# Layer 1 of a two-layer cross-attention kernel: two pairs of subtiles at a time, three of the seven half products split once more, softmax by head on ACT, in a fixed order

## The chip, the cores and the metric

The kernel runs on one core of a Trainium2 chip. A core has a matrix engine (TensorE, PE in the profile, with PEld for its weight loads), a vector engine (VectorE, DVE), a scalar engine (ScalarE, ACT), a general engine (GpSimd, POOL) and SyncE (SP), which here only issues transfers. Each engine runs its own instructions in order and waits on semaphores for the others. Operands lie in SBUF, matmul results in PSUM (eight banks of 512 float32 columns for 128 partitions). The metric is device time in microseconds, the median of several executions. One execution was also taken with the hardware profiler.

## The reference

Four batches of 1024 tokens of width 1024 go through two cross-attentions with 64 keys each. Cut to what matters:

```python
# layer 0: 32 query heads, 8 key heads of 32
out = softmax(q k^T / sqrt(32) + mask0) v          # 64 keys
x = layernorm((out @ Wo + bo) + x) * gamma0 + beta0
# layer 1: 16 heads of 64
a = layernorm(ctx) * gamma1 + beta1
scores = (x @ Wq.T) (a @ Wk.T)^T / 8               # 64 keys for each head, masked
out = softmax(scores) (a @ Wv.T) @ Wo.T
y = x + tanh(gate) * out
```

All of it is float32. As there are 16 heads of 64 keys, the scores of a token are again 1024 numbers. For each batch b the kernel folds Wq with the keys into one matrix ad[b] (1024 x 1024) and the values with Wo and the gate into bd[b] (1024 x 1024). Layer 1 is then, for 128 tokens at a time: s = x ad[b] + key_bias, a softmax over each of the 16 groups of 64 columns, and y = x + p bd[b].

## The kernel before

The 4096 tokens are 32 subtiles of 128, taken as 16 pairs. After layer 0's attention (to 681.5 us) comes layer 0's output projection, one pair after the other ("the wo stage", 681.5 to 1126.3 us), and then layer 1 (1126.3 to 1905.4 us): for each pair a score project with ad and an output project with bd.

A project multiplies 256 tokens x 1024 by 1024 x 1024 with the Strassen-Winograd scheme: the left side is four blocks of 128 tokens x 512, the right side four of 512 x 512, and seven block products take the place of eight. The left sums S1 to S4 are made by `left_out` (L429 to L432, four DVE additions of 128 x 512), the right sums T1, T2, T3, N4 by `right_sums` (L183 to L186, DVE, 128 x 2048) once for each batch. `products` (L446 the matmuls) makes each product as four K-steps of 128 x 128 x 512; the trace shows two PE records for each K-step, so 8 records a product and 56 a project. DVE takes each product from PSUM into the rows r or s (L455; L459 where the key bias is added). Products that share a bank go on adding to it after DVE has taken what it held: order X1, X6, V7, X5, X3, V4, W2, with four banks "wx" (128 x 512) and two double banks "big".

`project` puts a list of other steps ("fill") between the seven products: softmax steps, turns of the next rows, right sums. A scheduler then orders each engine's instructions, and can move PE's matmuls past one another.

The softmax of a subtile is `softmax_front` (L493 row maximum by head, L498 its floor, L501 subtraction, all on DVE, and L502 one exponential of 128 x 1024 on ACT) and `softmax_back` (L511 sum and L512 reciprocal by head, L516 division, on DVE). The rows are stored to p1 in DRAM on ACT's queue and come back as pq in a layout of quarters (`load_quarters`, ACT's queue), which DVE turns in 32 x 32 blocks (`turn_quarters`, L419). The rows x of layer 1, written to x1 in DRAM by `close_rows` of the wo stage (layer normalisation L292 to L309), come back on SP's queue as xq and are turned likewise. Pairs 0 and 15 of p are turned at once by PE transposes instead (L407) with ACT copies (L414). y is stored on SP's queue.

In the wo stage, POOL adds bo to the residual rows of each pair (L962), except for the first ones, which DVE does (L1099); bo is loaded in `other_work`, during layer 0's attention.

Of the kernel before, what the change touches and what calls it, by code (L numbers as in the profile page):

```python
# [14 lines left out]
P = 128  # L15
# [56 lines left out]
def tile_two_cross_attentions(  # L72
# [35 lines left out]
    ps_wx = ctx.enter_context(tc.tile_pool(name="ps_wx", bufs=4, space=bass.MemoryType.PSUM))  # L108
    ps_big = ctx.enter_context(tc.tile_pool(name="ps_big", bufs=2, space=bass.MemoryType.PSUM))
# [133 lines left out]
    mask1_sb = constant(mask1.partition_broadcast(P), [P, B, S], "mask1", U8)  # L243
# [401 lines left out]
    def load_queries(t):  # L645
        q = qpool.tile([P, KC, P], F32, tag="q", name=f"q0_{t}")
        nc.sync.dma_start(out=q, in_=qTd[t // SUB][:, :, sub_ap(t % SUB)])

        m = small.tile([P, 2, S], F32, tag="m0", name=f"m0_{t}", bufs=2)
        for e in range(2):  # L650
            nc.sync.dma_start(out=m[:, e], in_=mask0[sub_ap(t), :])
        queries[t] = q, m
# [313 lines left out]
    def other_work(rows):  # L966

        nonlocal fold, early, bo_sb, w_o, first, first_rows, second
# [20 lines left out]
        bo_sb = constant(bo0.partition_broadcast(P), [P, H], "bo", F32, fold)  # L989
# [50 lines left out]
    def open_stage():  # L1040
        nonlocal lpool, o2pool, rpool, gamma0_sb, beta0_sb
# [5 lines left out]
        gamma0_sb, beta0_sb = (  # L1047
            constant(ap.partition_broadcast(P), [P, H], n, F32, c2)
            for ap, n in ((gamma0, "gamma0"), (beta0, "beta0"))
# [16 lines left out]
    lefts = {}  # L1066

    def load_x1(pair):
        xq = xqpool.tile([P, 2 * NQ, QW], F32, tag="xq", name=f"xq1_{pair}")
        load_quarters(xq, x1[pair])  # L1070
        return xq

    def turn_x1(pair, xq, pool=None, tag="xT"):

        xT = (pool or xTpool).tile([P, KC, 2 * P], F32, tag=tag, name=f"xT_{pair}")

        def half(h):
            turn_quarters(xq, xT[:, h * HK : (h + 1) * HK, :], (h * HK, (h + 1) * HK))

        def blocks():  # L1080
            lefts[pair] = left_out(xT, lpool if pool else lxpool, f"x_{pair}")

        return [lambda: half(0), lambda: half(1), blocks]
# [18 lines left out]
    for pair in range(1, NPAIR):  # L1102
# [7 lines left out]
        if pair == KC + 2:  # L1110
            w_a, w_a_sums = right_weight(ad[0], "wb", "a0", True)
        if pair in (NPAIR - 3, NPAIR - 2):
            fill += w_a_sums[0:2] if pair == NPAIR - 3 else w_a_sums[2:4]
        if pair == 3:
            early_cm.close()
            xTpool = open_pool(last_cm, "x1T", 1)
            lxpool = open_pool(last_cm, "leftx", 1)
            xqpool = open_pool(last_cm, "x1q", 1)
        if pair == NPAIR - 4:
            xq = load_x1(1)  # L1120
        if pair == NPAIR - 3:
            fill += turn_x1(1, xq)

        def tail():
# [3 lines left out]
            else:  # L1128
                turned[2]()
# [3 lines left out]
        if pair == NPAIR - 2:  # L1133
            xq = load_x1(0)
            turned = turn_x1(0, xq, o2pool, "o2")
            fill = turned[:2] + fill
    w_b, w_b_sums = right_weight(bd[0], "wa", "b0", True)
    xq = load_x1(2)
    run(fill)
    stage.close()  # L1140


    spool = open_pool(last_cm, "scores1", 4)
    pqpool = open_pool(last_cm, "p1q", 1)
    scores = {}

    def score(pair, fill):
        if pair:
            s = [spool.tile([P, H], F32, tag="s", name=f"s1_{pair}_{u}") for u in range(2)]
        else:  # L1150
            both = o2pool.tile([P, 2, H], F32, tag="o2", name="s1_0")
            s = [both[:, u] for u in range(2)]
        project(lefts.pop(pair), w_a, s, fill, key_bias[:, pair // PPB, :])
        scores[pair] = [su.rearrange("p (h s) -> p h s", s=S) for su in s]

    def softmax1(pair):

        s = scores[pair]
        steps = []
        if pair in (0, NPAIR - 1):  # L1160
            at_once[pair] = pqpool.tile([P, 2, H], F32, tag="pq", name=f"pn_{pair}")
        for u in range(2):
            steps += softmax_front(s[u], True, f"1_{pair}_{u}", pair == 0)
        for u in range(2):
            total, divide = softmax_back(
                s[u], f"1_{pair}_{u}", at_once[pair][:, u] if pair in at_once else None
            )

            def end(u=u, total=total, divide=divide):
                total()  # L1170
                divide()
                if pair not in at_once:
                    nc.scalar.dma_start(
                        out=p1[pair][sub_ap(u), :], in_=s[u].rearrange("p h s -> p (h s)")
                    )

            steps.append(end)
        return steps

    def new_pT(pair):  # L1180
        return ppool.tile([P, KC, 2 * P], F32, tag="pT", name=f"pT1_{pair}")

    def turn_at_once(pair):
        pT = new_pT(pair)
        del scores[pair]
        for u in range(2):
            turn(at_once[pair][:, u], pT[:, :, sub_ap(u)])
        return left_out(pT, lppool, f"p_{pair}")

    probs1 = {}  # L1190
    at_once = {}

    def turn_p(pair):

        scores.pop(pair)
        pq = pqpool.tile([P, 2 * NQ, QW], F32, tag="pq", name=f"pq_{pair}")
        load_quarters(pq, p1[pair], nc.scalar)
        pT = new_pT(pair)

        def half(h):  # L1200
# [100 lines left out]
```

## Time and profile before

Runs: 1908.11, 1907.85 and 1911.4 us, median 1908.11. The profiled execution is one further execution; its span from first to last instruction is 1909.7 us, 1.6 us (0.1%) over that median, so its own time is taken as the span.

| stretch | us | PE busy | DVE busy | ACT busy | POOL busy | granted PE clock |
|---|---|---|---|---|---|---|
| whole span of the profiled execution | 1909.7 | 1865.5 | 1290.2 | 427.4 | 178.5 | 0.994 |
| wo stage, 681.5 to 1126.3 | 444.8 | 436.9 | 289.9 | 56.9 | 78.4 | 1.00 |
| layer 1, 1126.3 to 1905.4 | 779.1 | 777.6 | 508.1 | 39.3 | 0.0 | 1.00 |
| middle of layer 1, 1200 to 1600 | 400.0 | 400.0 | 263.4 | 16.9 | 0.0 | 1.00 |

How to read the lines below: the page's first part has each engine's busy time, its share of the span and its instructions. The chain has the work that ended last, followed backwards: a piece's start, its duration, engine, tile, line, and how many instructions it joins. A group has line, engine, operation, output and input tiles with shapes, and the count; after the bar busy time and mean ns of one; after the next the idle time of the engine just before them and what ended it. A line's own answer gives minimum, median and maximum ns. A window row gives its length and each engine's busy time with instructions in brackets, then granted clock, DMA share and GB/s. A DMA row gives the queue, count, KB of each transfer and the median us from issue to landing.

### The profile page before, as it was taken

The numbers are of one execution on the slowest core, as the hardware profiler recorded it, in microseconds if no ns is written. First come the engines' busy times: TensorE is split into PE (matmuls) and PEld (weight loads), VectorE is DVE, ScalarE is ACT, GpSimd is POOL, SyncE is SP. The second block draws the span as 40 slices with busy tenths as digits, with TensorE's granted clock in tenths as the row PEclk, the third lists the DMA queues.
The fourth block names the chain that finished last, engine by engine and source line by source line (L and its number), as shares of the span: only waits on it lengthen the run. The fifth ranks groups of instructions, "written<-read, shape, count | busy, mean of one in ns | idle before, by whom it ended". The sixth has DMA issues, their size and how long they took to land.

```text
span 1909.7 us, 17518 instructions
## 1 busy us (share of the span) xinstructions
PE 1865.5 (98%) x6096; PEld 879.6 (46%) x6096; DVE 1290.2 (68%) x1582; ACT 427.4 (22%) x1396; POOL 178.5 (9%) x212
## 2 busy tenths in 40 slices
PE   8999999999998899999999999999999999999999
PEld 7744444444445653343344444444444444444444
DVE  3425589789888985575568668557665766576653
ACT  1101575766546741212200001000000000000000
POOL 0016011111101003121113100000000000000000
PEclk9999999999999899999999999999999999999999
DMA  8996599998868965667473362466656565656421
GB/s 278 184 222 192 159 266 241 272 248 272 250 178 290 305 234 173 196 201 242 167 215 136 121 149 82 110 165 162 146 143 165 154 155 143 165 145 164 121 88 44
DMA packets 220745, 350.54 MB, mean 184 GB/s; under 512 B 26992, under 2 KB 146160, under 8 KB 215664
## 3 DMA queue, kind: packets, MB, share of 16 engines
q1 hardware_dynamic: 152896, 242.44, 45.8%
q0 software_dynamic: 15216, 60.83, 10.4%
q10 hardware_dynamic: 52544, 46.14, 8.7%
q8 instruction: 48, 0.79, 0.2%
q14 instruction: 41, 0.34, 0.1%
HBM read 207.53 MB, written 141.82 MB: 183 GB/s over the span
## 4 chain that ended last, share of the span: by engine, by line
PE 80%; DVE 9%; DMA 5%; ACT 3%; issue 2%; POOL 0%; SPq 0%; DVEq 0%; ACTq 0%; POOLq 0%
PE wx L446 59%; PE wx L576 12%; ACT s L698 2%; PE big L680 2%; DVE s L684 2%; PE wx L379 1%; PE big L379 1%; PE big L928 1%; DVE mx L691 1%; DVE s L715 1%; DMA q<-qTd 1%; DMA pq<-p 1%; DMA p<-s 1%; PE big L759 1%; DVE sm L711 1%
## 5 line engine op out<-in xcount | busy, mean ns | idle before, releaser
L455 DVE TENSOR_TENSOR r<-wx,r 128x512 f32<-128x512 f32 x224 | 153.3, 685 | 234.1 <-PE wx L446 218.1
L698 ACT ACTIVATE s<-s,mx 128x64 f32<-128x64 f32 x488 | 162.7, 336 | 80.4 <-DVE mx L691 77.3
L502 ACT ACTIVATE s<-s 128x1024 f32<-128x1024 f32 x32 | 33.7, 1057 | 651.7 <-DVE s L501 651.6
L459 DVE TENSOR_TENSOR s<-wx,key_bias 128x512 f32<-128x512 f32 x64 | 44.1, 689 | 136.8 <-PE wx L446 136.8
L446 PE MATMUL wx<-wo_B,S 128*128 128x512 f32 x256 | 116.8, 599 | 1.5 <-DVE r L455 1.5
L576 PE MATMUL wx<-xT,wq_S 128*128 128x512 f32 x256 | 116.6, 598 | 0.8 <-ACT z L587 0.8
L446 PE MATMUL wx<-b_B,pT 128*128 128x512 f32 x256 | 115.8, 593 | 0.6 <-ACT pT L414 0.6
L446 PE MATMUL wx<-b_B,S_p 128*128 128x512 f32 x256 | 116.0, 596 | 0.0
L446 PE MATMUL wx<-a_B,xT 128*128 128x512 f32 x256 | 115.4, 592 | 0.0
L446 PE MATMUL wx<-a_B,S_x 128*128 128x512 f32 x256 | 115.3, 593 | 0.1
L446 PE MATMUL wx<-wo_B,o 128*128 128x512 f32 x256 | 114.8, 596 | 0.0
L576 PE MATMUL wx<-xB,wq_A 128*128 128x512 f32 x256 | 113.7, 594 | 0.0
L962 POOL TENSOR_TENSOR r<-r,bo 128x1024 f32<-128x1024 f32 x30 | 77.7, 2597 | 317.7 <-DMA r<-in_x_dram 240.5
L680 PEld LDWEIGHTS big<-kv,q 64*128 64x128 f32 x1024 | 69.6, 194 | 49.2 <-issue 41.3
L684 DVE TENSOR_TENSOR s<-big,m 128x1024 f32<-128x1024 f32 x64 | 77.5, 1215 | 21.6 <-PE big L680 21.2
L698 ACT ACTIVATION_READ_ACCUMULATOR s<-s,mx 128x1 f32 x488 | 91.8, 188 | 0.0
L680 PE MATMUL big<-kv,q 64*128 64x128 f32 x1024 | 81.7, 291 | 1.9 <-DMA q<-qTd 1.8
L419 DVE STREAM_TRANSPOSE pT<-pq 128x1024 f32<-128x1024 f32 x66 | 78.0, 1219 | 5.0 <-DMA pq<-p 4.9
L446 PEld LDWEIGHTS wx<-wo_B,S 128*128 128x128 f32 x256 | 47.2, 190 | 67.7 <-issue 52.1
L715 DVE TENSOR_TENSOR s<-s,sm 128x1024 f32<-128x1024 f32 x64 | 77.0, 1216 | 0.9
L299 ACT ACTIVATE rstd<-rstd 128x1 f32<-128x1 f32 x32 | 6.5, 203 | 316.1 <-DVE rstd L298 316.1
L446 PEld LDWEIGHTS wx<-wo_B,o 128*128 128x128 f32 x256 | 47.8, 190 | 63.5 <-issue 62.4
(162 smaller groups left out, 2936.3 us busy)
## 6 DMA issues: line engine op xcount, KB each, us to landing
p<-s POOLq DMA_DIRECT2D x19, 1024.0 KB, 8.1
pq<-p POOLq DMA_DIRECT2D x76, 256.0 KB, 6.1
xq<-in_x_dram SPq DMA_DIRECT2D x64, 256.0 KB, 9.9
q<-qTd SPq DMA_DIRECT2D x32, 512.0 KB, 7.3
oTd<-oT ACTq DMA_DIRECT2D x32, 512.0 KB, 7.6
ad<-a POOLq DMA_DIRECT2D x16, 1024.0 KB, 8.6
o<-oTd SPq DMA_DIRECT2D x16, 1024.0 KB, 5.3
r<-in_x_dram SPq DMA_DIRECT2D x32, 512.0 KB, 5.3
```

Source lines behind the costliest of these rows:

```text
L379: nc.tensor.matmul(ps[:, 0:256], w[k // HK, c // HK][:, k % HK, sub_ap(c % HK)], ct[:, k, :], start=(k == 0), stop=(k == KC - 1),)
L419: return nc.vector.transpose(dst.rearrange("p k (u i) -> p k u i", i=Q), t[:, :, k0 * Q : k1 * Q].rearrange("p u (k j) -> p k u j", j=Q),)
L446: nc.tensor.matmul(banks[name], a[s][:, k, :], w[m][:, k, :], start=first and k == 0, stop=last and k == HK - 1, skip_group_check=True,)
L455: nc.vector.tensor_tensor(at, bank, at, ALU.add)
L459: nc.vector.tensor_tensor(at, bank.rearrange("p (h s) -> p h s", s=S), bias.unsqueeze(1).to_broadcast([P, 512 // S, S]), ALU.add,)
L502: nc.scalar.activation(s, s, AF.Exp)
L576: nc.tensor.matmul(bank, w_q[a][:, k, sub_ap(i)], rows[b][:, k, :], start=first and k == 0, stop=last and k == HK - 1, skip_group_check=True,)
L680: nc.tensor.matmul(ps[:, at : at + P], q[on, c * 4 + g, :], k0bd[on, b, c, :], start=True, stop=True,)
L684: nc.vector.tensor_tensor(quarters[:, :, c * 8 : (c + 1) * 8], ps.rearrange("p (k a l) -> p a k l", a=NQ, l=Q), mask.rearrange("p e (h l) ...
L698: nc.scalar.activation(heads[:, e, k], heads[:, e, k], AF.Exp, bias=mx[:, e, k : k + 1], accum_out=sm[:, e, k : k + 1],)
L715: nc.vector.tensor_tensor(heads[:, e], heads[:, e], wide(sm[:, e]), ALU.mult)
L962: nc.gpsimd.tensor_tensor(ru, ru, bo_sb, ALU.add)
```

## The change

- Layer 1 goes by quads, two pairs P and Q at a time: 8 quads, a score phase and an output phase for each, in the order written (`manual_schedule`: the scheduler moves nothing). PSUM is opened anew: two wx banks and three double banks.
- Products 1, 6, 7, 5 of each pair stay whole (line 1202). Products 2, 3 and 4 use the same right block for P and Q, so each becomes a "joint" (a, b, c) of 256 tokens x 512 by 512 x 512, done with the same scheme once more: seven half products of two K-steps x 256 columns (line 1285), with sums of 128 x 512 right blocks and 128 x 256 left blocks on POOL (lines 1273 and 1277), 12 of each in a phase. All half products of a joint use one double bank (V, W, X within it). The takes are lines 1295 and 1299. Three half products of joint a or b of a phase (`REST`) are done after the first product of the next phase, and b3 after its second.
- The last output phase is plain (14 whole products).
- `go` writes each phase: PE in the order `MIX`, and after each product the takes and as much of the planned fill (DVE steps with a planned time and a duration, loads with a time) as fits; what is left over is written at the end of the phase.
- Softmax: DVE has the negated maximum (1384, 1385); ACT does 16 exponentials by head with the maximum as its bias, which also give the sums (1387); DVE the reciprocal (1392); ACT 16 copies with a scale (1397), and the store on its queue (1398). In the first and last quad ("soon") DVE divides (1394) and SP stores. All pairs go through p1 in DRAM; no PE transposes are left.
- Rows are loaded one subtile at a time (transfers of 128 KB, line 261, two buffers) all on SP, turned in halves (426), and summed (1107 to 1113). Pair 1's rows of x are loaded at the start of layer 1, where they were loaded three pairs before the end of the wo stage.
- bo is loaded when the wo stage opens. mask1 and the m0 masks move to other pools; other pools close earlier.

```diff
-        bo_sb = constant(bo0.partition_broadcast(P), [P, H], "bo", F32, fold)
...
-        gamma0_sb, beta0_sb = (
+        bo_sb, gamma0_sb, beta0_sb = (
             constant(ap.partition_broadcast(P), [P, H], n, F32, c2)
-            for ap, n in ((gamma0, "gamma0"), (beta0, "beta0"))
+            for ap, n in ((bo0, "bo"), (gamma0, "gamma0"), (beta0, "beta0"))
...
+            x_left, loads, turns, sums = turned_rows(x1[0], "x0")
+            run(loads)
...
+        def load(u):
+            rows.append(load_rows(src, u, queue))
+
+        def half(u, h):
+            if not left:
+                left["ta"] = lapool.tile([P, HK, 2 * P], F32, tag="Ta", name=f"ta_{name}")
+                left["tb"] = lp.tile([P, HK, 2 * P], F32, tag="Tb", name=f"tb_{name}")
+            turn_quarters(
+                rows[u], left["tb" if h else "ta"][:, :, sub_ap(u)], (h * HK, (h + 1) * HK)
+            )
+
...
+        sums = [
+            sum1,
+            lambda: tt(room("S2", lapool), left["S1"], left["A11"], ALU.subtract),
+            lambda: tt(left["S3"], left["A11"], left["S3"], ALU.subtract),
+            lambda: tt(room("S4", lp), left["A12"], left["S2"], ALU.subtract),
+        ]
...
+    ps_wx = open_banks("ps_wx1", 2)
+    ps_big = open_banks("ps_big1", 3)
...
+    BIG, INNER = 3.43, 0.86
+    JOINT = {"a": ("A12", "B21", 0, 0), "b": ("S4", "B22", 0, 1), "c": ("A22", "N4", 1, 0)}
+    MIX = (
+        "P1 | P6 cT1 cT2 cT3 cN4 aT1 aT2 | P7 P5 Q1 "
+        "cS1 cS2 cS3 cS4 aS1 aS2 c1 c2 Q6 c6 aT3 aS3 Q7 c7 aN4 aS4 Q5 c4 bT1 c5 bS1 bT2 "
+        "a1 a2 c3 bS2 a6 bT3 bS3 b1 a7 bN4 bS4 b2 b6 a4 a5 b7"
+    ).split()
+    REST = ["a3 b4 b5".split(), ["b3"]]
+    PLAIN = "P1 | P7 P6 | P2 P5 P4 P3 Q1 Q7 Q6 Q2 Q5 Q4 Q3".split()
...
+        def product(key, i, s, m, first, last):
+            if first:
+                banks[key, i] = ps_big.tile([P, 1024], F32, tag="big", name="w")[:, 0:512] if key == "W" else wx()
+            for k in range(HK):
+                nc.tensor.matmul(
+                    banks[key, i], left[i][s][:, k, :], w[m][:, k, :],
+                    start=first and k == 0, stop=last and k == HK - 1, skip_group_check=True,
+                )
...
+        table = {
+            "1": ("X", "A11", "B11", True, False, [(0, 0)]),
+            "6": ("X", "S2", "T2", False, False, [(1, 0)]),
+            "7": ("V", "S3", "T3", True, joint, [(1, 1), (1, 0)] if joint else [(1, 1)]),
+            "5": ("X", "S1", "T1", False, joint, [(1, 1), (0, 1)] if joint else [(1, 1)]),
+        }
...
+            def rsum(o, x, y):
+                rb[o] = jrpool.tile([P, 2, 256], F32, tag="jr", name=f"{o}_{j}")
+                nc.gpsimd.tensor_tensor(rb[o], rb[x], rb[y], ALU.subtract)
+
+            def lsum(o, x, y, op):
+                lb[o] = jlpool.tile([P, 2, P], F32, tag="jl", name=f"l{o}_{j}")
+                nc.gpsimd.tensor_tensor(lb[o], block(x), block(y), op)
+
+            def mm(key, a, b, first, last):
+                if not ps:
+                    t = ps_big.tile([P, 1024], F32, tag="big", name="joint")
+                    ps["all"] = t.rearrange("p (b o) -> p b o", o=256)
+                    ps["V"], ps["W"], ps["X"] = t[:, 0:256], t[:, 256:512], t[:, 512:768]
+                for k in range(2):
+                    nc.tensor.matmul(
+                        ps[key], block(a)[:, k, :], rb[b][:, k, :],
+                        start=first and k == 0, stop=last and k == 1, skip_group_check=True,
+                    )
...
+            for name, args, takes in (
+                ("1", ("X", "A11", "B11", True, False), [(one, lambda: take("X", 0, 0))]),
+                ("2", ("W", "A12", "B21", True, True), []),
+                ("6", ("X", "S2", "T2", False, False), [(one, lambda: take("X", 1, 0))]),
+                ("7", ("V", "S3", "T3", True, False), [(one, lambda: take("V", 1, 1))]),
+                ("4", ("V", "A22", "N4", False, True), []),
+                ("5", ("X", "S1", "T1", False, False), [(pair, lambda: take_two(1, slice(0, 4, 2)))]),
+                ("3", ("X", "S4", "B22", False, True), [(pair, lambda: take_two(0, slice(1, 3)))]),
+            ):
+                steps[j + name] = (INNER, lambda args=args: mm(*args), takes)
...
+        def put(until, tol):
+            nonlocal taken
+            for f in [f for f in fill if len(f) > 3 and f[3] <= until]:
+                fill.remove(f)
+                taken += f[1]
+                f[2]()
+            n = 0
+            while n < len(fill):
+                t, d, f, *_ = fill[n]
+                if t <= until - BIG / 2 and (not d or max(taken, until - BIG) + d <= until + tol):
+                    taken = max(taken, t) + d if d else taken
+                    f()
+                    fill.pop(n)
+                elif d or t > until:
+                    break
+                else:
+                    n += 1
+
+        def do(name, steps):
+            nonlocal at, taken
+            d, mm, takes = steps[name]
+            mm()
+            if not d:
+                return
+            at += d
+            put(at, 1.0 if d == BIG else 0.7)
+            taken = max(taken, at)
+            for d, take in takes:
+                take()
+                taken += d
...
+        for f in fill:
+            f[2]()
...
+        def front():
+            nc.vector.tensor_reduce(mx, v, AX.X, ALU.max, negate=True)
+            nc.vector.tensor_scalar(mx, mx, -LEAST_MAX, None, ALU.min)
+            for h in range(16):
+                nc.scalar.activation(
+                    v[:, h], v[:, h], AF.Exp, bias=mx[:, h : h + 1], accum_out=sm[:, h : h + 1]
+                )
+
+        def back():
+            nc.vector.reciprocal(sm, sm)
+            if soon:
+                nc.vector.tensor_tensor(v, v, sm.unsqueeze(2).to_broadcast([P, 16, S]), ALU.mult)
+            else:
+                for h in range(16):
+                    nc.scalar.activation(v[:, h], v[:, h], AF.Copy, scale=sm[:, h : h + 1])
+            (nc.sync if soon else nc.scalar).dma_start(out=to, in_=s[:, u])
+
+        return front, back
...
+        D = 0.2
+        return [
+            (0.5, F, f0), (10.4, F, f1), (12.5, D, b0), (19.0, F, f2), (23.0, D, b1), (27.6, F, f3), (37.0, D, b2)
+        ], [(5.0, D, b3)]
...
+    def turn_steps(kind, q, i, t_load, t_turn, end=99.0):
+        src = (x1 if kind == "x" else p1)[2 * q + i]
+        left, loads, turns, sums = turned_rows(src, f"{kind}_{q}_{i}")
+        lefts.setdefault((kind, q), [None, None])[i] = left
+        return [(t_load, 0.0, f) for f in loads], [(t_turn, 0.7, f, end) for f in turns] + [
+            (t_turn, 0.85, f, end) for f in sums
+        ]
...
+    def weight(w, tag, name):
+        r, loads = right_loads(w, tag, name, True)
+        t1, t2, t3, n4 = right_sums(r)
+        return r, [(10.6, 0.0, f) for f in loads], [(29.0, 2.3, t1), (29.1, 2.3, t2)], [
+            (0.0, 2.4, t3, 9.0), (0.1, 2.4, n4, 9.0)
+        ]
...
+    def score(q, fill):
+        scores[q] = new_rows(f"s1_{q}")
+        go(
+            phase(lefts["x", q], w_a, scores[q], key_bias[:, q // QPB, :]), fill,
+            after_rest=(lambda: store(q - 2, 0)) if q > 1 else None,
+        )
...
+    l, t = turn_steps("x", 0, 1, 0.0, 0.0, 13.5)
+    fill = l + t
+    l, t = turn_steps("x", 1, 0, 12.0, 17.3)
+    fill += l + t
+    l, x_late = turn_steps("x", 1, 1, 24.0, 0.0, 13.5)
+    fill += l
+    score(0, fill)
...
+    for n in range(NQUAD):
+        if 0 < n < NQUAD - 1:
+            q = n + 1
+            fill = x_late + a_late + sm_late + [(0.0, 0.0, lambda n=n: store(n - 1, 1))]
+            a_late, sm_late = [], []
+            l, t = turn_steps("p", n, 0, 8.0, 17.3)
+            fill += l + t
+            l, p_late = turn_steps("p", n, 1, 24.0, 0.0, 13.5)
+            fill += l
+            fill += loads_of_rows(n, 15.0, 19.0)
+            if n % QPB == 0:
+                w_b, l, t, b_late = weight(bd[n // QPB], "wa", f"b{n // QPB}")
+                fill += l + t
+            score(q, fill)
+        if n == NQUAD - 1:
+            break
+        fill = p_late + b_late
+        p_late, b_late = [], []
+        now, sm_late = softmax_steps(n + 1, n + 2 == NQUAD)
+        fill += now
+        if n + 2 < NQUAD:
+            l, t = turn_steps("x", n + 2, 0, 8.0, 17.3)
+            fill += l + t
+            l, x_late = turn_steps("x", n + 2, 1, 24.0, 0.0, 13.5)
+            fill += l
         else:
...
+            l, t = turn_steps("p", n + 1, 0, 26.0, 32.0)
+            fill += l + t + loads_of_rows(n + 1, 30.0, 42.0)
+            l, p_late = turn_steps("p", n + 1, 1, 43.0, 0.0, 13.5)
+            fill += l
+        if (n + 2) % QPB == 0 and n + 2 < NQUAD:
+            w_a, l, t, a_late = weight(ad[(n + 2) // QPB], "wb", f"a{(n + 2) // QPB}")
+            fill += l + t
+        go(phase(lefts["p", n], w_b, residual[n], None), fill)
+    n = NQUAD - 1
+    fill = p_late + [(0.0, 0.0, lambda: store(n - 1, 1))]
+    go(phase(lefts["p", n], w_b, residual[n], None, False), fill, PLAIN, lambda: store(n - 1, 0))
+    store(n, 1)
+    store(n, 0)
```

## The prediction

> **What bounds the kernel now.** I read the page's first and fourth parts (who is busy, which chain ended last), then the chain in order of time, then the two stages in a table by windows, then groups and DMA landings for prices.
>
> ```profile
> span 1909.7 us, 17518 instructions
> PE 1865.5 (98%) x6096; PEld 879.6 (46%) x6096; DVE 1290.2 (68%) x1582; ACT 427.4 (22%) x1396; POOL 178.5 (9%) x212
> PE 80%; DVE 9%; DMA 5%; ACT 3%; issue 2%; POOL 0%; SPq 0%; DVEq 0%; ACTq 0%; POOLq 0%
> ```
> ```profile
> 31.50 3.45 PE big L379 x16
> ...
> 710.04 6.66 DMA r<-in_x_dram
> 720.14 5.41 PE wx L446 x8
> 733.10 3.70 PE wx L446 x8
> ...
> 1181.70 696.98 PE wx L446 x1616
> 1880.70 24.70 PE wx L446 x56
> ```
> ```profile
> 681.50:1126.30 444.80, 436.90 (x1105) 182.80 (x1105) 289.90 (x416) 56.94 (x120) 78.44 (x31) 1.00 0.55 177
> 1126.30:1905.40 779.10, 777.63 (x1825) 341.37 (x1823) 508.07 (x647) 39.26 (x39) 0.00 (x0) 1.00 0.53 137
> ```
>
> Layer 1 lies between 1126.3 and 1905.4 us, and one unbroken run of 1616 PE records fills nearly all of it. PE is the bound there: DVE is busy for 508 of 779 us (65%), ACT for 39, POOL for none. So arithmetic taken from PE is worth its full price, but only while whatever feeds PE stays on time. The prices come from these rows:
>
> ```profile
> L455 DVE TENSOR_TENSOR r<-wx,r 128x512 f32<-128x512 f32 x224 | 153.3, 685 | 234.1 <-PE wx L446 218.1
> L698 ACT ACTIVATE s<-s,mx 128x64 f32<-128x64 f32 x488 | 162.7, 336 | 80.4 <-DVE mx L691 77.3
> L698 ACT ACTIVATION_READ_ACCUMULATOR s<-s,mx 128x1 f32 x488 | 91.8, 188 | 0.0
> L419 DVE STREAM_TRANSPOSE pT<-pq 128x1024 f32<-128x1024 f32 x66 | 78.0, 1219 | 5.0 <-DMA pq<-p 4.9
> ```
> ```profile
> L379 PE MATMUL wx<-ctxT,wk x64: 379/379/483, 27.3 to 51.8; 128*128 128x256 f32 x64
> L520 DVE TENSOR_TENSOR pn<-s,sm x16: 412/416/419, 1168.0 to 1866.6; 128x256 f32<-128x256 f32 x16
> L429 DVE TENSOR_TENSOR S<-o x16: 673/680/2840, 647.8 to 1093.4; 128x512 f32<-128x512 f32 x16
> ```
> ```profile
> xq<-x SPq DMA_DIRECT2D x64, 256.0 KB, 7.1
> out_dram<-r SPq DMA_DIRECT2D x32, 512.0 KB, 5.5
> p<-s ACTq DMA_DIRECT2D x28, 512.0 KB, 2.7
> wq<-in_wq_dram SPq DMA_DIRECT2D x32, 128.0 KB, 3.2
> ```
>
> **PE's arithmetic: a gain.** A 512-column record costs 696.98 / 1616 = 0.431 us, a product of eight 3.45. Sixteen 256-column records take 3.45, so one is 0.216 and a half product (four) 0.86. Two pairs cost 14 x 3.45 = 48.3 us before; after, 8 x 3.45 + 21 x 0.86 = 45.7. The last output phase stays plain: 15 x 2.6 = **-39**. What layer 1 spent beyond its 32 x 24.15 us of records, 779.1 - 772.9 = 6.2, was PE's 64 transposes for pairs 0 and 15 and the exposed turns around them; these go: **-6**.
>
> **A wait written into the joints: certain.** Half product 2 follows 1 directly in joints c and a. In the built order its first matmul waits for DVE's take of half product 1, since both write one tile. That costs a last record that ends after its pitch (0.379 - 0.216 = 0.16), DVE's start (0.04), the 128x256 take (0.416) and PE's restart with an exposed weight load (0.15): 0.76 us. In joint b, a7 lies between. 2 x 15 x 0.76 = **+23**. Half of the gain is lost with it.
>
> **What I cost at nothing, and its cover.** Powers by head: 16 x (0.24 pitch + 0.09) = 5.3 us of ACT for a subtile, four subtiles and three divisions of 3.2 in an output phase: 31 of 45.7, beside PE; without that slack DVE's reciprocals and p's stores would run late by the excess. The wx banks fall from four to two: a bank is refilled one product (3.45) after its last write and DVE's take is 0.69 or 1.22, so about 2 us are to spare; uncovered, up to 1.5 a product. The loads of p rows leave ACT's queue for SP's, and halve in size: some 28 issues of 0.45 are 13 us in a phase, hidden unless one of them waits (next). The masks' pools and earlier closings move no instruction of layer 0.
>
> **The written order of DVE against late rows.** DVE's work in a phase: takes of eight full products 4 x 0.69 + 4 x 1.22 (1024 columns) = 7.6; of three joints 3 x (3 x 0.42 + 2 x 0.69) = 7.9; four maxima (1.20 + 0.17) 5.5; two sets of turned rows 2 x (4 x 0.61 + 4 x 0.685) = 10.4. Output phases add parts of a third set (5.2), and in n = 0, 2, 4 two weight sums at the start and two at the end (rows of 128x2048: 2.28 each, 9.1). With the reciprocals that is 46.4 against 45.7 of PE, before any wait. The plan's own figures are a little higher, so something is pushed past the phase's end. By the built order it is the division of the third subtile, T1 and T2 of the next batch's a, and the loads of the last x rows (planned at 24 us). Those loads use completion semaphores handed out in turn to SP's and ACT's transfers, eight in all: one load waits for the store of p on ACT's queue. Chain: last take, two weight sums 4.6, reciprocal 0.24, sixteen ACT copies of 64 columns, store 2.7, issue 0.4, load 3.2 (128 KB row) to 7.1 (256 KB row), remaining transposes and first sum 1.9, P1's take 0.7. ACT's copies have no row: above is the power with its accumulator (16 x 0.33 = 5.3), below nothing; I take 3.2, 0.2 each, the 128x64 size and no accumulator. Sum 17 to 21. PE has only P1, a3, b4, b5 (3.45 + 3 x 0.86 = 6.0) before P6, which adds into P1's bank and so waits for that take: 17 to 21 less 6 is 11 to 15, and I take the low end, 11, since the last products' tail covers some of the sums; scores 2, 4, 6: **+33** (bounds +15 to +45).
>
> In the same phases SP issues four y stores only after the take of b3, then p rows, again behind those semaphores (store 5.5, load 3.2 or more). DVE's turns of p stand at 17 us of the plan, ahead of c1's take, for which c2 waits. Store 5.5 + two rows' loads 3.2 + three SP issues 1.2, less the few us by which the turns were due later: about 9 each, **+28** (0 to +40). In n = 0, 2, 4 the b weights' T3 and N4 (4.6) precede c1's take: 4 each, **+12** (0 to +14).
>
> **Ends of the stage.** Pair 1's x rows are now loaded behind the last store of layer 0. DVE's normalisation ran to 1136.2 before; load 3.2 to 7.1, turns 2.4 and the take 0.7 then precede P6, which could start at 1129.8: 11. Output 0 needs p rows just stored (divide 1.2, store 2.7, load 3.2 to 7.1, turns 2.4): 10. The last quad likewise, less what its products cover: 4 + 7. Divides on DVE in score 1, three of 1.2: 4. Together **+36** (0 to +55). bo is now loaded when the wo stage opens: its 6.0 us and POOL's 2.35 us additions move behind it and reach the takes of pair 1: **+9** (0 to +12).
>
> **POOL and DVE.** POOL had nothing in layer 1; now 12 sums of 512 columns and 12 of 256. By L962 (2354 ns for 1024 columns of two sources) 1.2 and 0.6: 22 us of 45.7. In the wo stage L429 reached 2840 ns from 680 beside such an addition, while L455, with a PSUM source, kept 685. Seven to ten two-source DVE operations in a phase can each wait up to 1.2: +4 in the phases where DVE has no slack is already in the bounds above; elsewhere I take nothing, since DVE ends some 5 us early. If not, up to 15 x 3 = +45. [...]
>
> **Clock.** At 720.14 eight records took 5.41 instead of 3.63 after 2.24 us of idle PE (granted 0.50 from 722 to 724): 1.8 lost. Some 11 stalls above 4 us: 11 x 1.8 = **+20** (0 to +30). [...]
>
> **Sum** on the profiled execution (span 1909.7; 1.6 over the median of the runs, 1908.1, which is 0.1%): -39 - 6 + 23 + 33 + 28 + 12 + 36 + 9 + 20 = +116. From the median 2024; I give 2020.
>
> **Rivals.** *The arithmetic wins* (other side): loads land early enough that no phase waits for rows. Then -45 + 23 = -22: 1886, or 1895 with bo's 9. For it: DMA share is only 0.53, POOL and ACT have been idle. Against it: the order makes the x loads follow a store that follows the weight sums, however fast the transfers. It decides where the chain of 17 to 21 us shrinks to P1's 6. *Stalls half as large*: transfers of 128 KB near 2 us, the copies near 0.1 us each, DVE catching up; half of 33 + 28 + 12 + 36, clock +8: -22 + 55 + 9 + 8 = +50, 1958. *DVE becomes the bound through POOL*: the +45 on top, 2065. *The clock stays full*: without the 20, 2000, inside the likeliest.
>
> **How the numbers follow.** Likeliest (2020, its own range 1985 to 2055) 0.58; half stalls (1925 to 1985) 0.22; POOL lock (2055 to 2100) 0.10; arithmetic wins 0.08 faster; 0.02 for no change. Under 1935 and over 2070 I leave about 0.2. Runs of this kernel tell about 0.2% (3.8 us) from no change.
>
> **What would show it.** Right: in the chain of layer 1, pieces of PE of about 45 us between DMA rows into xq and turns (L426); P6 waiting 10 us at scores 2, 4, 6; c2 and a2 waiting 0.7 us on L1295 thirty times; records of 256 columns at 0.216; granted clock under 1 after the stalls; bo's load inside 690 to 720. Wrong: PE's waits in layer 1 under 40 us in total, or the waits on POOL rather than on DVE and DMA. The forecast fails most likely through DMA latencies, of which seven chains hang on two or three in a row.

## The result and the profile after

The changed kernel takes 2022.6 us (median of four runs, 2021.1 to 2027.3), the kernel before 1909.8 on the same chip: a ratio of **1.0596, 95% interval 1.058 to 1.0613**. The profiled execution has a span of 2020.4 us against 1909.7, so 110.7 us have to be found.

The page after: the first two lines of its busy part, the granted clock in fortieths of the span, and the shares of the chain that ended last.

```profile
span 2020.4 us, 20947 instructions
PE 1860.1 (92%) x6604; PEld 989.3 (49%) x6604; DVE 1332.7 (66%) x1717; ACT 654.8 (32%) x2768; POOL 552.9 (27%) x572
PEclk9999999999998999999999898989998999899999
PE 62%; DVE 15%; DMA 12%; ACT 5%; issue 4%; SPq 2%; POOL 0%; DVEq 0%; ACTq 0%; POOLq 0%
```

PE is busy for 92% of the span instead of 98%, and on the chain it falls from 80% to 62%. No engine has taken its place: DVE stands at 66%, ACT at 32%. The missing time is idle PE, and dips of the clock behind it.

Layer 1 alone, in the table by windows (length, busy time of PE, weight load, DVE, ACT and POOL, granted clock, DMA share, GB/s):

```profile
1132.80:2016.00 883.20, 771.09 (x2334) 451.82 (x2332) 548.07 (x785) 266.50 (x1411) 371.77 (x358) 0.94 0.47 125
```

PE's busy time is 771 us where it was 778, though 39 us of arithmetic went: busy time counts a slowed matmul in full (a record of 592 ns reaches 1222), and the clock of the stage is 0.94 instead of 1.00. By its first record layer 1 starts at 1133.27 instead of 1126.33 (+6.9), and the other 103.8 us come after that. PE's waits from the wo stage on (us in total, times, longest):

```profile
PE wx L1202 <- DVE s L1215: 46.3, 4, 11.7
PE joint L1285 <- DVE s L1295: 23.0, 16, 4.8
PE wx L1202 <- DVE r L1213: 21.7, 5, 12.2
PE joint L1285 <- DVE r L1295: 19.4, 14, 4.0
PE wx L453 <- DVE r L462: 7.5, 5, 2.8
```

Without the last, which lies in the wo stage, and with one short wait of 1.5 more, layer 1 waits 112 us. L1202 is a full product, L1285 a joint; L1215, L1213 and L1295 are DVE's takes. P6 below is product 6 of pair P, c2 half product 2 of joint c, and so on. PE's timeline shows where (start, length, instruction, and in brackets the idle time before it and what ended it):

```profile
1148.59 5.77 PE L1202 MATMUL wx<-a_T,S_x 128*128 128x512 f32 x8 [11.72 <-DVE s L1215]
1262.44 5.17 PE L1202 MATMUL wx<-b_T,S_p 128*128 128x512 f32 x8 [12.17 <-DVE r L1213]
1445.82 1.13 PE L1285 MATMUL joint<-a_N,tb_x 128*128 128x256 f32 x4 [0.52 <-DVE s L1295]
1497.04 1.63 PE L1285 MATMUL joint<-b_N,tb_p 128*128 128x256 f32 x4 [3.88 <-DVE r L1295]
1541.40 5.63 PE L1202 MATMUL wx<-a_T,S_x 128*128 128x512 f32 x8 [11.48 <-DVE s L1215]
1563.46 2.07 PE L1285 MATMUL joint<-a_N,tb_x 128*128 128x256 f32 x4 [4.41 <-DVE s L1295]
1971.67 5.53 PE L1202 MATMUL wx<-b_T,S_p 128*128 128x512 f32 x8 [8.23 <-DVE r L1213]
```

One of each kind: the start of the layer, output 0, the wait written into a joint, the b sums in an output phase, P6 and then c2 in score 4, and the last quad. Score 4 is where the forecast's longest chain stands, so here is the chain of waits in order of time (start, length, what):

```profile
1517.83 3.13 DMA p<-s
1520.97 3.29 DMA a_B<-ad
1524.28 2.29 DVE a_B L190
...
1528.80 0.25 DVE sm L1392
...
1529.08 1.10 ACT s L1397 x5
...
1530.29 2.73 ACT s L1397 x11
1533.04 2.61 DMA p<-s
1535.67 0.30 SPq L261
...
1536.02 2.57 DMA xq<-x
...
1538.71 0.71 DVE ta_x L426
...
1540.66 0.68 DVE s L1215
```

A store of p, then SP's queue at the load's line, then the load of the last x row, its turn, and the take for which P6 waits. The load goes out when a store of another tensor on ACT's queue has landed (1535.65; the load's line starts at 1535.67); that the two share a semaphore is the forecast's reading of the program, and the trace shows only this order. One step earlier the same stands once more: the first weight sum (L190) waited for a weight load that followed a store of p.

### The profile page after: what moved, and what is told of

Its sections match the earlier page's. It is cut to its first block, busy times and chain, and to the rows that moved or that the text cites. A ratio compares the mean times of both kernels' runs of the same rounds, so it can differ in the third digit from the quotient of the medians.

```text
span 2020.4 us, 20947 instructions
## 1 busy us (share of the span) xinstructions
PE 1860.1 (92%) x6604; PEld 989.3 (49%) x6604; DVE 1332.7 (66%) x1717; ACT 654.8 (32%) x2768; POOL 552.9 (27%) x572
## 4 chain that ended last, share of the span: by engine, by line
PE 62%; DVE 15%; DMA 12%; ACT 5%; issue 4%; SPq 2%; POOL 0%; DVEq 0%; ACTq 0%; POOLq 0%
PE wx L453 18%; PE wx L583 13%; PE wx L1202 13%; PE joint L1285 9%; DMA xq<-p 2%; ACT s L1387 2%; PE big L687 2%; DMA p<-s 2%; DMA r<-x 2%; DVE s L691 1%; PE wx L386 1%; PE big L386 1%; DMA b_B<-bd 1%; PE big L935 1%; ACT s L1397 1%
## 5 line engine op out<-in xcount | busy, mean ns | idle before, releaser
L1387 ACT ACTIVATE s<-s,mx 128x64 f32<-128x64 f32 x512 | 170.1, 334 | 427.4 <-DVE mx L1385 373.3
L705 ACT ACTIVATE s<-s,mx 128x64 f32<-128x64 f32 x488 | 162.7, 336 | 80.2 <-DVE mx L698 77.1
L462 DVE TENSOR_TENSOR r<-wx,r 128x512 f32<-128x512 f32 x112 | 76.7, 686 | 144.9 <-PE wx L453 139.6
L1397 ACT ACTIVATE s<-s,sm 128x64 f32<-128x64 f32 x384 | 94.1, 334 | 99.7 <-DVE sm L1392 99.7
L1202 PE MATMUL wx<-a_T,S_x 128*128 128x512 f32 x128 | 71.3, 708 | 46.3 <-DVE s L1215 46.3
L1387 ACT ACTIVATION_READ_ACCUMULATOR s<-s,mx 128x1 f32 x512 | 95.8, 187 | 0.0
L705 ACT ACTIVATION_READ_ACCUMULATOR s<-s,mx 128x1 f32 x488 | 91.8, 188 | 0.0
L746 POOL DMA_DIRECT2D pq<-p x76 | 41.5, 553 | 164.7 <-DVE pT L426 57.7
L1202 PE MATMUL wx<-b_T,S_p 128*128 128x512 f32 x128 | 65.2, 657 | 21.7 <-DVE r L1213 21.7
L1215 DVE TENSOR_TENSOR s<-wx,key_bias 128x512 f32<-128x512 f32 x64 | 43.7, 683 | 62.2 <-PE wx L1202 58.7
```

What stands on the lines that cost most here:

```text
L462: nc.vector.tensor_tensor(at, bank, at, ALU.add)
L705: nc.scalar.activation(heads[:, e, k], heads[:, e, k], AF.Exp, bias=mx[:, e, k : k + 1], accum_out=sm[:, e, k : k + 1],)
L1202: nc.tensor.matmul(banks[key, i], left[i][s][:, k, :], w[m][:, k, :], start=first and k == 0, stop=last and k == HK - 1, skip_group_check= ...
L1387: nc.scalar.activation(v[:, h], v[:, h], AF.Exp, bias=mx[:, h : h + 1], accum_out=sm[:, h : h + 1])
L1397: nc.scalar.activation(v[:, h], v[:, h], AF.Copy, scale=sm[:, h : h + 1])
```

## Experiments

The first four runs ask which part of the change costs what. The kernel before has a median of 1908.7 us beside them, and of 1910.1 and 1909.2 us on the two other chips used below; so ratios to it are given with each time.

**Half product 2 moved apart from half product 1.** Joints c and a start with another product between the two that share a tile.

```
-        "cS1 cS2 cS3 cS4 aS1 aS2 c1 c2 Q6 c6 aT3 ...
-        "a1 a2 c3 bS2 a6 ...
+        "cS1 cS2 cS3 cS4 aS1 aS2 c1 Q6 c2 c6 aT3 ...
+        "a1 c3 bS2 a2 a6 ...
```

> In the order of the joints, another product is put between half products 1 and 2: c1 Q6 c2, and a1 c3 a2. Theory (a wait written into the order, its own cost): the 30 waits of joints on L1295 go, each 0.52 us of idle PE and 0.27 of a slow first record; where DVE is behind anyway (c2 at 1349, 1563, 1779 with 4.4 to 4.8, at 1282, 1497, 1712 with 2.5 to 3.9) the wait moves on to Q6 and stays. 30 x 0.79 = 24, less some 4 where c3 comes close behind a take: 20 less, 2002 us. Rival (DVE is the bound, through POOL or its own work, and these waits only show its lag): under 6 less, 2017 or more.

Measured: 2008.3 us, ratio 1.0517 (1.0495 to 1.0538), 14 us less than the change, or 15 by the two ratios (0.79% of 1908.7). Of the thirty waits on L1295 one of 0.6 us is left; the four longest lines of PE's table in layer 1 are now:

```profile
PE wx L1202 <- DVE s L1215: 58.1, 7, 11.8
PE wx L1202 <- DVE r L1213: 31.0, 8, 11.7
PE joint L1285 <- DVE r L1299: 3.4, 1, 3.4
PE joint L1285 <- DVE s L1299: 2.5, 1, 2.5
```

But eight of them had become longer waits for late rows or a late DVE, and those stayed, now mostly before Q6 (4.04, 4.18 and 3.57 us in scores 2, 4 and 6, where c2 had 4.82, 4.41 and 4.65). So the 22 joints that waited for the tile alone should return 22 x 0.79 = 17; 15 arrived, well over the rival's bound of 6. The wait written into the joints is real, and it is not the main cost.

**The x rows of layer 1 loaded on POOL's queue.** By the forecast's reading of the program this takes the x loads out of the semaphores that SP's loads share in turn with ACT's stores; the order of DVE, its work and the stores stay.

```
-        left, loads, turns, sums = turned_rows(src, f"{kind}_{q}_{i}")
+        left, loads, turns, sums = turned_rows(src, f"{kind}_{q}_{i}", nc.gpsimd if kind in 'x' else nc.sync)
```

> The rows of x are loaded from POOL's queue and not from SP's, so that they no longer take turns with the stores of p at the eight completion semaphores; all else is the same. Theory (the last x load of an output phase stands behind a store of p, which stands behind two weight sums): the waits of P6 at 1326, 1541 and 1756 (11.5 us each) fall to about 4, as the reciprocal 0.2, ACT's copies 3.9 and the store 2.2 leave the chain, and PE's clock recovers 1 us each: 25 less, 1997 us. Rival (transfers are late by themselves, or DVE is): within 4 us of 2022.6. Second rival (POOL is what is short): slower, as 8 issues of 0.55 us in a phase delay its sums.

Measured: 2000.1 us, ratio 1.0484 (1.0467 to 1.0501): 22 us less than the change. P6's waits at scores 2, 4 and 6 fall from 11.5 us to 2.89 each (3 x 8.6 = 26), while c2's in outputs 0, 2 and 4 grow by 1.4 to 1.7. P6 and c2 in PE's timeline of this kernel in score 4:

```profile
1530.04 6.68 PE L1202 MATMUL wx<-a_T,S_x 128*128 128x512 f32 x8 [2.89 <-DVE s L1215]
1552.99 1.97 PE L1285 MATMUL joint<-a_N,tb_x 128*128 128x256 f32 x4 [4.25 <-DVE s L1295]
```

With DVE's order and work untouched, three quarters of the P6 wait go when the load no longer stands on SP's queue behind a store. The queue and the semaphore were moved together; the runs don't part them. Nor is the load's place enough by itself, as the next run shows.

**All phases of layer 1 as 14 whole products.** No joints and no POOL sums; the smaller pools, the ACT powers and division, the rows by 128 and DVE's written order stay. The wx banks go back to four, and P2 stands between P1 and P6.

```
-    ps_wx = open_banks("ps_wx1", 2)
-    ps_big = open_banks("ps_big1", 3)
+    ps_wx = open_banks("ps_wx1", 4)
+    ps_big = open_banks("ps_big1", 2)
...
-    PLAIN = "P1 | P7 P6 | P2 ...
+    PLAIN = "P1 | P2 P6 | P7 ...
...
-    def go(steps, fill, order=MIX, after_rest=None):
+    def go(steps, fill, order=PLAIN, after_rest=None):
...
-            phase(lefts["x", q], w_a, scores[q], key_bias[:, q // QPB, :]), fill,
+            phase(lefts["x", q], w_a, scores[q], key_bias[:, q // QPB, :], False), fill,
...
-        go(phase(lefts["p", n], w_b, residual[n], None), fill)
+        go(phase(lefts["p", n], w_b, residual[n], None, False), fill)
```

> Every phase with 14 whole products, no joints and no sums on POOL; four wx banks and two double ones; quads, softmax on ACT, loads and the rest as in the changed kernel. Theory (the joints fill DVE's phase: 46.4 us of work in 45.7 where a batch changes, against 40.5 in 48.3 here): PE's arithmetic comes back, +39, the joints' waits go, -24, the waits of 11.5, 4.5 and 3.9 at the batch changes go, -35 -12 -9, some 15 at the ends, and 20 of clock: 1947 us, 1915 to 1965. Rival (the loads are late by the order and the transfers, whoever computes): only +39 - 24, 2038 us.

Measured: 1934.6 us, ratio 1.0132 (1.0115 to 1.0148). PE's waits in layer 1 are 22 us instead of 112:

```profile
PE wx L1202 <- DVE s L1215: 13.3, 4, 8.7
PE wx L1202 <- DVE r L1213: 5.1, 2, 3.1
PE wx L1202 <- DVE a_T L192: 2.7, 3, 0.9
PE wx L1202 <- DVE b_T L192: 1.0, 1, 1.0
```

So the joints, with the order in which they stand, their sums on POOL and the two banks, cost 88 us on balance, though they take 39 us of arithmetic away. The softmax on ACT is not what is slow: without the joints' takes DVE has room in its phase, and the same softmax fits.

The x load stands here where it stands in the change, and the chain of score 4 is the same one: store of p at 1484.07, issue, load, turn, take. Yet P6 waits only 1.73 us there (1.48, 1.73 and 1.39 in scores 2, 4 and 6). From the start of P1 to the start of P6 in score 4 it is 17.66 us in the change, 9.08 with the x loads on POOL's queue and 8.76 here. So the load behind the store costs 8.6 us only where the joints have made DVE, and the store with it, late; taking away either is enough.

**The same with POOL's 24 sums computed and read by nobody.** It does the work of the sums without their use, to price POOL beside DVE.

```
+        "P1 | P2 P6 cT1 cT2 cT3 cN4 aT1 aT2 | P7 P5 P4 cS1 cS2 cS3 cS4 aS1 aS2 P3 Q1 aT3 aS3 Q7 aN4 aS4 "
+        "Q6 bT1 bS1 bT2 Q2 bS2 bT3 bS3 Q5 bN4 bS4 Q4 Q3"
...
-        if not joint:
-            return steps
```

> As the plain kernel, and POOL computes the 24 sums of a phase all the same, in the places they had, with nobody reading them. It measures what POOL's sums cost DVE and PE by themselves. Theory (small: in the changed kernel L1107 to L1113 took 27 us more than 685 ns each over the whole stage, 2 us in a phase, and DVE has 8 us to spare in a plain phase): 0 to 10 us more than plain. Rival (POOL makes DVE the bound): 30 to 45 us more than plain.

Measured: 1947.2 us, ratio 1.0201 (1.0186 to 1.0216): +12.6 on the kernel above, just over the theory's 10 and far under the rival's 30 to 45. The groups of DVE in layer 1, by line (busy us, mean ns of one), without POOL's sums:

```profile
L1112 DVE TENSOR_TENSOR ta_x<-ta_x 128x512 f32<-128x512 f32 x15 | 10.3, 686 | 0.0
L1113 DVE TENSOR_TENSOR S_x<-tb_x,S_x 128x512 f32<-128x512 f32 x15 | 10.3, 686 | 0.0
```

and with them:

```profile
L1112 DVE TENSOR_TENSOR ta_x<-ta_x 128x512 f32<-128x512 f32 x15 | 19.9, 1325 | 0.0
L1113 DVE TENSOR_TENSOR S_x<-tb_x,S_x 128x512 f32<-128x512 f32 x15 | 18.7, 1249 | 0.0
L1218 DVE TENSOR_TENSOR s<-wx,key_bias 128x512 f32<-128x512 f32 x64 | 44.1, 688 | 91.9 <-PE wx L1205 82.1 <-issue 6.1 <-DMA x<-r 3.7
```

These two sums, of rows in SBUF, take nearly twice as long (686 ns to 1325 and 1249); the other groups of 128x512 sums of turned rows go from 682 to 691 ns to 740 to 1057. The take from PSUM has 688 ns, and 690 without POOL's sums.

**Joints only where there is room.** From the kernel so far, joints (apart) are kept in scores 2 to 7 and outputs 1, 3, 5, nine phases; the other phases are plain; wx has four banks, and product 2 uses them too; the first phase has an order of its own; the weights' late sums are due sooner (6.5 instead of 9.0).

```
-            (0.0, 2.4, t3, 9.0), (0.1, 2.4, n4, 9.0)
+            (0.0, 2.4, t3, 6.5), (0.1, 2.4, n4, 6.5)
...
+            phase(lefts["x", q], w_a, scores[q], key_bias[:, q // QPB, :], q in (2, 3, 4, 5, 6, 7)), fill,
+            MIX if q in (2, 3, 4, 5, 6, 7) else PLAIN if q else FIRST_ORDER,
...
+        go(phase(lefts["p", n], w_b, residual[n], None, n in (1, 3, 5)), fill, MIX if n in (1, 3, 5) else PLAIN)
```

> Joints only where DVE has room: scores 2 to 7 and outputs 1, 3, 5; the other phases (where a batch's sums, the first and the last rows fall) have 14 whole products. The joints' order is that of joints_apart; four wx banks, two double ones, product 2's bank from wx; T3 and N4 one product earlier; the first phase does P2 and P7 before P6. Theory (the joints cost time only where they overfill DVE): plain's 1934.6 less 9 phases x 2.6 = 23 of arithmetic, less 3 of the first wait, plus some 6 of waits in the joint phases: 1914 us, 1905 to 1925. Rival (any phase with joints and POOL's sums loses what it saves): 1930 to 1945.

Measured: 1928.8 us, ratio 1.0093 (1.0077 to 1.0108). That is 4 us above the expected range and just under the rival's. P6 waits 4.83, 3.90 and 3.70 us at scores 2, 4 and 6, and the chain of waits at score 2 names the same cause as in the change:

```profile
1293.32 2.61 DMA p<-s
1295.94 0.30 SPq L261
...
1296.29 2.61 DMA xq<-x
...
1300.97 0.69 DVE s L1216
```

**The same, retimed.** bo is loaded at its old place into a pool of its own, and the times of the written plan are moved so that loads come ahead of the stores they stood behind; a batch's first two weight sums come 6 us earlier as well.

```
+        bo_sb = constant(bo0.partition_broadcast(P), [P, H], "bo", F32, bopool)
...
-            (0.5, F, f0), (10.4, F, f1), (12.5, D, b0), (19.0, F, f2), (23.0, D, b1), (27.6, F, f3), (37.0, D, b2)
+            (0.5, F, f0), (10.4, F, f1), (13.2, D, b0), (18.3, F, f2), (26.6, D, b1), (27.1, F, f3), (37.0, D, b2)
...
-        return r, [(10.6, 0.0, f) for f in loads], [(29.0, 2.3, t1), (29.1, 2.3, t2)], [
+        return r, [(12.3, 0.0, f) for f in loads], [(23.1, 2.3, t1), (23.2, 2.3, t2)], [
...
-            l, t = turn_steps("x", n + 2, 0, 8.0, 17.3)
+            l, t = turn_steps("x", n + 2, 0, 5.8, 18.9)
...
-            l, x_late = turn_steps("x", n + 2, 1, 24.0, 0.0, 13.5)
+            l, x_late = turn_steps("x", n + 2, 1, 17.9, 0.0, 7.9)
...
-            l, t = turn_steps("p", n + 1, 0, 26.0, 32.0)
+            l, t = turn_steps("p", n + 1, 0, 26.0, 38.9)
```

> As room, with bo loaded at its old place (its own small pool) and with planned times moved: the batch's first two weight sums from 29 to 23 us, the late x rows' loads from 24 to 18, other steps by up to 7 us. Theory: 5 less for bo, and the waits of P6 at the batch changes (1.5 to 3 us each with what the clock loses) less by half, 6 or so: 11 less than room; by the estimate for room 1903 us, which is 0.3% under the kernel before. Rival (the times of the plan matter little as long as the order of loads stays): room less 5, 1909.

Measured: **1899.7 us** (1896.4 to 1902.6), ratio to the kernel before **0.9942, 0.9929 to 0.9955**: a little faster than the kernel before (0.6%), and 123 us faster than the change. It is 29 us less than the kernel above, where 11 were expected: bo is worth 7 (next run), PE's waits in layer 1 fall from 24 to 11 us, and three of four stalls that cost clock are gone. What the moved loads and the earlier sums give separately was not tried. P6 waits 1.07 us at scores 2, 4 and 6. The busy part of its page and PE's waits in layer 1:

```profile
PE 1838.6 (97%) x6388; PEld 935.1 (49%) x6388; DVE 1290.3 (68%) x1655; ACT 654.1 (35%) x2768; POOL 414.2 (22%) x428
```
```profile
PE wx L1207 <- DVE s L1220: 8.9, 5, 4.9
PE wx L1207 <- DVE r L1218: 1.3, 1, 1.3
PE wx L1207 <- DVE b_T L192: 0.9, 1, 0.9
```

**Only bo's load moved back**, in the changed kernel:

```
-            for ap, n in ((bo0, "bo"), (gamma0, "gamma0"), (beta0, "beta0"))
+            for ap, n in ((gamma0, "gamma0"), (beta0, "beta0"))
...
+        bo_sb = constant(bo0.partition_broadcast(P), [P, H], "bo", F32, bopool)
```

> The changed kernel with bo loaded at its old place, in layer 0's attention; all else the same. Theory: the wo stage, 450.0 us against 444.8, gets its 5.2 back: 2017 us. Rival (the 5 us come from the other moves, of pools and of the rows of x): within 2 of 2022.6.

Measured: 2015.6 us, ratio 1.0553 (1.0532 to 1.0573): 7 to 8 us less than the change. Layer 1 starts at 1126.1 instead of 1133.3, where the kernel before starts it at 1126.3. So the whole shift ahead of layer 1 is bo's.

**The retimed kernel without joints**, and **with joints in more phases** (also score 1 and outputs 0, 2, 4, 6), to see what the joints are worth once rows come in time:

```
+            phase(lefts["x", q], w_a, scores[q], key_bias[:, q // QPB, :], q in ()), fill,
```
```
+            phase(lefts["x", q], w_a, scores[q], key_bias[:, q // QPB, :], q in (1, 2, 3, 4, 5, 6, 7)), fill,
```

> room_retimed with no joints: 14 whole products in all 16 phases; the plan's times, bo's place and the banks stay. It prices the joints in nine phases by themselves. Theory (PE's arithmetic counts in full where nothing else is late): 1899.7 + 9 x 2.6 = 1923 us, less up to 4 for waits that the joint phases still have. Rival (the times of the plan did it all, and the joints earn nothing): 1900 us.

> room_retimed with joints in the other phases too: score 1 and outputs 0, 2, 4, 6 (score 0 and the last output stay plain). Theory (where a batch changes, and at the ends, the joints leave no time for DVE's sums and the rows' round trips): 5 x 2.6 = 13 of arithmetic saved, but waits of 5 to 12 us come back at each of outputs 0, 2, 4, 6 or the score after it, with clock: 40 to 60 more than room_retimed, 1940 to 1960 us. Rival (only the order of loads and stores mattered, and the new times mended it): 1887 us.

Measured: 1915.2 us without joints, ratio 1.002 (1.0009 to 1.0032), 4 us under the expected range; 1957.7 with joints in more phases, ratio 1.024 (1.0217 to 1.0263). So nine phases with joints are worth 0.78%, 15 us, of the 9 x 2.6 = 23 that their arithmetic saves; the phases added cost 57 us more than they save (2.98% of 1910). In the kernel with more joints P6 waits 9.27, 9.48 and 9.21 us again at scores 2, 4 and 6, and output 0 waits 13.2:

```profile
PE wx L1207 <- DVE s L1220: 35.2, 6, 9.5
PE wx L1207 <- DVE r L1218: 23.5, 5, 13.2
PE wx L1207 <- DVE ta_p L428: 5.1, 2, 2.6
```

The long waits lie in and behind outputs 0, 2 and 4, the output phases that also hold two weight sums at each end. In score 4 P6 waits 9.48 us, up to 1511.27, again for DVE's take (L1220), retimed or not. Five phases were added at once, so what each costs isn't parted; and joints in more phases with the x loads on POOL's queue were not tried, so these phases are shown not to fit only with the loads where they are.

## Why the prediction was right, step by step

The time (2020 foretold, 2022.6 measured) and the sum (+116 foretold, +110.7 measured) agree, but two of the terms were missed in opposite directions. Against the trace, the terms that came out smaller fall short by 21 us in all and those that came out larger exceed by 14. That these nearly cancel is luck; the path is not. Each term against the trace after:

| term | foretold | measured | read from |
|---|---|---|---|
| PE's arithmetic, 15 phases | -39 | -39 | 40 joint records in 8.90 us, 0.27 of it the slow first: 0.216 each |
| transposes and exposed turns | -6 | -6 | gone from PE; the size is that of the rows before |
| joints' own wait | +23 | +23.7 | 30 x (0.52 idle + 1.13 - 0.86) |
| P6 at scores 2, 4, 6 | +33 | +34.6 | 11.49, 11.48, 11.64 |
| c2 in the same phases | +28 | +12.3 | 4.82, 4.41, 4.65, each less 0.52 |
| b sums in outputs 0, 2, 4 | +12 | +8.7 | 3.88, 3.88, 2.46, each less 0.52 |
| ends of the stage | +36 | +39.6 | 11.72 at the start; 1.50 + 2.43 in score 1; 12.17 in output 0; 3.51 in output 6; 8.23 in the last |
| bo and the wo stage | +9 | +6.9 | start of layer 1 |
| clock | +20 | +28 | PE's busy time times the missing clock, by 1-us windows |

The measured column gives +109; 2 us stay unassigned.

**Right by mechanism and size.** The price of the arithmetic and the wait written into the joints, where one tile serves both half products, came straight from rows of the trace, and the joints' records run at the foretold 0.216 us:

```profile
1182.30 8.90 PE joint L1285 x40
```

P6's chain is the one foretold, down to the semaphore: sums, reciprocal, ACT's copies, store, load, turn, take: 17.1 us in score 4 from the first weight sum to P6, where 17 to 21 were foretold. Its parts stood differently inside: sixteen ACT copies take 3.8 us (guessed 3.2; the group's mean is 334 ns against a pitch of 0.24), the row's load 2.6 (guessed 3.2 to 7.1), and the weight sum stood itself behind an earlier store, which the forecast did not have. The forecast named the semaphores as one link beside DVE's overfull order; the run with the x loads on POOL's queue shows that the load's place carries 8.6 of the 11.5 us, and the plain kernel that it does so only beside that overfull order.

**Mis-sized: c2.** The term "Store 5.5 + two rows' loads 3.2 + three SP issues 1.2 … about 9 each" measured 4.1. The y stores' issues take 2.9 us (four lines of SPq from 1548.77 to 1551.66) and two loads 4.92 and 4.40 follow, longer than foretold together. But the chain starts at the take of b3, and PE still has P7, P5, Q1 and c1 to do between b3 and c2, 3 x 3.43 + 0.86 = 11.2 us; the term took off only "the few us by which the turns were due later". P6's long stall has not paid for part of c2's, as the run with the x loads on POOL's queue shows: there P6 waits 8.6 us less, and c2 still 5.59, 4.25 and 4.32.

**Mis-sized: the clock.** +28 for 20. "11 x 1.8" undercounts: 14 stalls of PE cost clock, ten above 4 us and four of 2.46 to 3.88, at 2.0 each on average, and the short stalls cost no less than the long ones here (below). The retimed kernel has one such stall and loses 1.5 us.

**POOL beside DVE** was costed at nothing with a rival of up to +45. In the change it lengthens DVE's SBUF sums (L1113 to 1322 ns for x, 1196 for p, where 685 is undisturbed), some 27 us of DVE in the stage for L1107 to L1113; by itself, in the kernel without joints, POOL's work moved the time by 12.6 us. In the change it can't be separated from the terms above, since DVE's lateness is in all of them: zero as a term of its own was too kind, and the rival's +45 is more than three times what that kernel shows.

**The ends** were right in size. But at the start the take that P6 waits for follows the store of layer 0's last x rows (3.07 us, then the take at 1147.84), where the forecast had the load and turn of pair 1. Why the take needs that store was not tried. The 1.50 in score 1 is a wait of Q1 for a bank of wx, the one place where the two banks, costed at nothing, show; with four banks and joints in score 1 it is gone.

**The rivals.** That the arithmetic wins needed the loads to come free of the stores. That condition was the right one, with DVE's room as the second: where the plan allows both, in nine phases, the same arithmetic wins 15 us.

## What to carry to other kernels

Fewer matmul cycles pay only while every feeding engine still ends inside the shortened phase: add up each engine's work per phase, and give the saving only to phases with room (nine such phases gained 15 us here, five more lost 57). Look for a load that must come on time behind another queue's store; here moving the load, not speeding anything up, took 8.6 of 11.5 us off the wait. And put two products that share a PSUM tile one product apart where an engine must take the first before the second may write; thirty such places cost 15 us here.

## What the runs showed of the hardware that was not expected

**Every stall of PE from 2.86 us on cost clock here, and its length did not order how much.** PE's first product of eight records after a wait takes 3.70 us at full clock. In the traces of these kernels, from the wo stage on, no idle of PE of up to 2.00 us is followed by slower records, and every one from 2.86 us on is. Between 2.17 and 2.85 both occur, in one and the same kernel too; the first two rows are from the kernel with joints in more phases, the third from the plain kernel and the fourth from the one with unread sums:

```profile
1231.11 5.40 PE L1207 MATMUL wx<-b_B,ta_p 128*128 128x512 f32 x8 [2.56 <-DVE ta_p L428]
1892.73 3.70 PE L1207 MATMUL wx<-b_B,ta_p 128*128 128x512 f32 x8 [2.56 <-DVE ta_p L428]
1884.48 6.75 PE L1202 MATMUL wx<-b_T,S_p 128*128 128x512 f32 x8 [3.08 <-DVE r L1213]
1498.57 5.40 PE L1205 MATMUL wx<-a_T,S_x 128*128 128x512 f32 x8 [3.08 <-DVE s L1218]
```

Once clock is lost, it is 1.4 to 3.2 us in layer 1, counted from the starts of the products that follow, and the length of the idle doesn't order it: 3.08 us give 6.75 and 5.40, and so 11.89 (bo moved back) gives 6.61 and 12.17 (the change) 5.17. What decides between them the traces don't show. So the x loads on POOL's queue, which cut three waits by 8.6 us each to 2.89, saved no clock: 14 stalls cost it as before, 31 us in layer 1 by the same count, against 28. The shortest idle of PE with slower records behind it is 2.17 us (at 1272.06, in the kernel with joints in more phases), the longest without is 2.69 (at 1227.88, with bo moved back).

**POOL's sums and DVE's both ran longer side by side.** In the kernel with unread sums one group of POOL's 128x512 sums has a mean of 1789 ns and another 1536, where the fastest groups of the same size stand at 1265 to 1276 ns, while DVE's sums go from 686 to 1325 ns.
